# Softmax sums from ones beside the values, with head rows gathered by transfers, in a windowed attention and mixture-of-experts kernel

## The chip, the cores and the metric

The kernel runs on one core of a Trainium2 chip. TensorE multiplies matrices into PSUM, VectorE (DVE) and ScalarE (ACT) read PSUM and work on SBUF, GpSimd (POOL) works on SBUF and issues indirect transfers, SyncE (SP) issues the other transfers. The metric is the device time of one execution in microseconds, shown as the median of several runs.

## The reference

The input is 8 sequences of 1024 rows of 128 numbers. Cut to what matters:

```python
def attn(x, Wq, Wk, Wv, Wo):              # H = 16 heads of 8, window 64
    q, k, v = (split_heads(x @ w) for w in (Wq, Wk, Wv))
    scores = einsum('bhld,bhlwd->bhlw', q, k_win) * 8 ** -0.5   # row l sees rows l-63 .. l
    scores = where(invalid, -inf, scores)
    attn = softmax(scores, axis=-1)
    ctx = einsum('bhlw,bhlwd->bhld', attn, v_win)
    return ctx.reshape(Bx, Lx, 128) @ Wo

def ffn(x, w_router, w1, w2, bias):       # 8 experts, two of them for each row
    scores = softmax(xf @ w_router)
    expert_weights, top_experts = top_k(scores, 2)
    # rows go to their experts in order, up to a capacity of 2048 rows each
    h = gelu(einsum('ech,ehf->ecf', xb, w1))
    y = einsum('ecf,efh->ech', h, w2)
    return scatter_add(weight * y) + bias

x = x + attn(layernorm(x), Wq, Wk, Wv, Wo)
x = x + ffn(layernorm(x), w_router, w1, w2, bias)
```

What this change touches is the end of the attention: the product of the unnormalised probabilities P with the values (the numerators), the sums of P over the window (the denominators), and their quotient, ctx.

## The kernel before

A first phase computes attention and routing, a second one the experts; the second reads the rows that the first has scattered into the table xb, so it starts when the last of them has landed.

The first phase walks over 64 tiles of 128 rows: sequences b = 0 to 7, and in each tiles j = 0 to 7. Heads are held in four groups g of 32 partitions (a quad), four heads r to a quad. Iteration i of the loop at L1017 is one step; it does, in this order on each engine:

- scores of tile i+1 (L518 adds the mask, L534 the products), 128 rows x 96 columns for each head; then on DVE their maxima (L542) and two subtractions that split each maximum into BF16 pieces (L550);
- `attend` of tile i-1: 16 matmuls of P with the values (L620), 8 with a block of ones, obd, for the sums (L627). Both write one PSUM tile av. ScalarE copies it, keeping the even heads (L633), DVE adds the odd heads (L634), takes the reciprocal of the sums (L639) and multiplies (L640) into ctx;
- `probs` of tile i: masks (L579, L587), scores transposed (L596), then the turn of the maxima of tile i+1 (L559, copied by ScalarE at L561), then the subtraction of the maxima (L604) and the exponential on ScalarE (L610);
- the plan of this step: a list of calls written out by hand with `at(b, j, ...)` at L837 to L967. Among them are projections (`queries`, `keys`, `values`, `turn`) of the next sequence and the output projection, second normalisation and routing (`Piece`) of the sequence before. L904 `half` and L936 `piece` do the same for the two halves of the last two sequences.

The order on TensorE, DVE, ScalarE and POOL is the order in which the calls are written. SP's transfers are put into an order by the framework; a transfer that waits holds up those behind it on its queue. SP carries the loads of x, the spreading of queries and keys into their block layout (`spread`, L478 and L481), the copies of the values to the other half of the partitions (L467, L469) and the rows with bias (L704). POOL issues the indirect transfers to xb (`put`, L796), up to three in a step, each tied to a matmul of the step.

PSUM is tight: score tiles and probability tiles take turns in one pool of three buffers (ps_u, two tiles of each in a step); every other product (av, pm, projections) takes turns in a pool of two (ps_t).

After the loop the last tile is attended, the last two half sequences go through `piece`, the last rows are put, and 20 matmuls on the identity (L1049) stand before the expert phase.

## Time and profile before

| | |
|---|---|
| median of 15 runs | 767.72 us (765.59 to 769.61) |
| the profiled execution | 764.39 us |
| its span, first to last instruction | 762.5 us |
| mean granted TensorE clock | 0.962 |
| instructions | 23,372 |
| first expert products | 496 us |

Times inside the span are in microseconds from its start. Groups are listed by line, engine, operation and tiles (out<-in); after the count stand busy time, mean nanoseconds of one, and idle time of the engine just before them. In a timeline the columns are start, length, engine, line and operation, and in brackets the idle time before and what ended it; a merged row covers several instructions. FP32 matmuls are recorded as two instructions each, and matmuls of different quads run side by side, so the busy time of a group is less than its count by its mean.

### The profile page before, as it was taken

The numbers are of one execution on the slowest core, as the hardware profiler recorded it, in microseconds if no ns is written. First come the engines' busy times: TensorE is split into PE (matmuls) and PEld (weight loads), VectorE is DVE, ScalarE is ACT, GpSimd is POOL, SyncE is SP. The second block draws the span as 40 slices with busy tenths as digits, with TensorE's granted clock in tenths as the row PEclk, the third lists the DMA queues.
The fourth block names the chain that finished last, engine by engine and source line by source line (L and its number), as shares of the span: only waits on it lengthen the run. The fifth ranks groups of instructions, "written<-read, shape, count | busy, mean of one in ns | idle before, by whom it ended". The sixth has DMA issues, their size and how long they took to land.

```text
span 762.5 us, 23372 instructions
## 1 busy us (share of the span) xinstructions
PE 685.9 (90%) x9749; PEld 492.4 (65%) x9749; DVE 415.7 (55%) x1142; ACT 374.8 (49%) x665; POOL 394.8 (52%) x518
## 2 busy tenths in 40 slices
PE   8899999999999999999998872399999999999990
PEld 6455655655556546556555541389999999898990
DVE  6586778878888788888788777021111111111010
ACT  5465666675675666656655441023444444443430
POOL 7001030354543543444414556538778787787876
PEclk9999999999999999999999996689999999999995
DMA  2444445133123333232212111236455465463333
GB/s 79 128 143 144 148 141 187 36 98 98 48 88 98 92 94 93 88 90 66 83 58 56 47 45 60 81 92 107 50 113 106 46 123 94 52 119 34 37 32 30
DMA packets 66698, 65.25 MB, mean 86 GB/s; under 512 B 9043, under 2 KB 53944, under 8 KB 65696
## 3 DMA queue, kind: packets, MB, share of 16 engines
q1 hardware_dynamic: 39328, 38.08, 16.5%
q0 software_dynamic: 22528, 16.74, 15.5%
q10 hardware_dynamic: 4736, 8.93, 3.1%
q8 instruction: 77, 1.26, 0.7%
q14 instruction: 29, 0.24, 0.1%
HBM read 17.37 MB, written 29.88 MB: 62 GB/s over the span
## 4 chain that ended last, share of the span: by engine, by line
PE 65%; DVE 11%; POOL 8%; issue 7%; ACT 5%; DMA 3%; SPq 0%; POOLq 0%; ACTq 0%; DVEq 0%
PE yp L1118 11%; PE hp L1107 11%; PE av L620 7%; PE av L627 6%; PE t L596 6%; PE s L534 6%; POOL out_dram L1128 5%; ACT pr L610 3%; DVE mx L542 3%; PE pm L559 3%; PE s L518 2%; PE po L675 2%; PE pq L429 2%; PE t L604 2%; DMA out_dram<-ye,dest 2%
## 5 line engine op out<-in xcount | busy, mean ns | idle before, releaser
L1128 POOL DMA_INDIRECT out_dram<-ye,dest x128 | 198.6, 1552 | 68.4 <-issue 26.2
L796 POOL DMA_INDIRECT xb<-xn,si x128 | 126.4, 987 | 174.9 <-PE s L534 75.5
L542 DVE TENSOR_REDUCE mx<-s 128x8 f32<-128x768 f32 x128 | 116.5, 952 | 42.6 <-PE s L534 39.3
L1118 PEld LDWEIGHTS yp<-w,hT 128*128 128x128 f32 x1024 | 124.9, 193 | 9.1 <-ACT hT L1111 3.8
L1118 PE MATMUL yp<-w,hT 128*128 128x128 f32 x1024 | 126.2, 276 | 4.6 <-DVE ye L1123 3.9
L610 ACT ACTIVATE pr<-t 128x1024 f32<-128x1024 f32 x128 | 124.5, 1029 | 1.9 <-PE t L604 1.7
L1107 PE MATMUL hp<-xts,w 128*128 128x256 f32 (+1 forms) x528 | 123.3, 377 | 0.3 <-DVE xts L1098 0.3
L1123 DVE TENSOR_TENSOR ye<-yp,gt 128x256 f32<-128x256 f32 (+1 forms) x66 | 27.1, 415 | 162.7 <-PE yp L1118 122.7
L1111 ACT ACTIVATE hT<-hp 128x512 f32<-128x512 f32 x128 | 76.4, 597 | 71.8 <-PE hp L1107 66.9
L1107 PEld LDWEIGHTS hp<-xts,w 128*128 128x128 f32 x528 | 94.9, 194 | 10.1 <-DVE xts L1098 0.5
L620 PEld LDWEIGHTS av<-pr,vbd 128*32 128x32 f32 x2048 | 54.1, 110 | 47.1 <-issue 28.1
L620 PE MATMUL av<-pr,vbd 128*32 128x128 f32 x2048 | 73.4, 278 | 5.8 <-ACT pr L610 2.7
L633 ACT ACTIVATE own<-av,even 128x256 f32<-128x256 f32 x64 | 30.3, 474 | 94.1 <-PE av L627 94.1
L561 ACT COPY mxt<-pm 128x512 bf16<-128x512 bf16 x64 | 37.5, 586 | 78.4 <-PE pm L559 68.7
L596 PE MATMUL t<-qbd,kt 32*128 32x256 f32 x1024 | 69.6, 383 | 0.0
L627 PE MATMUL av<-pr,obd 128*32 128x256 f32 x1024 | 69.6, 383 | 0.0
L1098 ACT COPY xts<-xt 128x256 f32<-128x256 f32 (+1 forms) x57 | 21.0, 369 | 87.7 <-PE xt L1096 87.7
L639 DVE RECIPROCAL rd<-own 128x128 f32<-128x128 f32 x64 | 61.0, 953 | 2.2
L534 PE MATMUL s<-kbd,qt 32*32 32x384 f32 x2048 | 60.2, 493 | 1.4 <-issue 0.8
L596 PEld LDWEIGHTS t<-qbd,kt 32*128 32x128 f32 x1024 | 47.3, 187 | 3.3 <-issue 0.9
L518 PE MATMUL s<-ms,i 32*128 32x384 bf16 x256 | 34.2, 329 | 9.5 <-ACT pr L610 7.0
L627 PEld LDWEIGHTS av<-pr,obd 128*32 128x32 f32 x1024 | 35.7, 111 | 9.7 <-issue 0.7
(179 smaller groups left out, 782.1 us busy)
## 6 DMA issues: line engine op xcount, KB each, us to landing
xb<-zeros ACTq DMA_DIRECT2D x16, 528.0 KB
xe<-xb SPq DMA_DIRECT2D x7, 1056.0 KB
vbd<-vbd SPq DMA_DIRECT2D x32, 192.0 KB
kbd<-kt SPq DMA_DIRECT2D x62, 72.0 KB
qbd<-qt SPq DMA_DIRECT2D x64, 64.0 KB
out_dram<-x SPq DMA_DIRECT2D x32, 128.0 KB
w<-in_L_ffn_w_dram SPq DMA_DIRECT2D x16, 256.0 KB
x<-in_L_attn_x_dram SPq DMA_DIRECT2D x22, 128.0 KB
```

What stands on the lines that cost most here:

```text
L534: done = nc.tensor.matmul(place(g, slice(32 * blk, 32 * (blk + 1))), lhsT=qt[quad(g), q0 : q0 + 32], rhs=kbd[quad(g), :, c0 + 32 * blk : c ...
L542: nc.vector.tensor_reduce(out=part_of(mx, 0)[:, 2 * u : 2 * u + 2], in_=units[u][:, :, 0 : 4 * KB].rearrange("p g (r k) -> p g r k", r=4), ...
L596: nc.tensor.matmul(units[g // 2][:, g % 2, w], lhsT=kt[quad(g), q0 : q0 + P], rhs=qbd[quad(g), :, c0 : c0 + 64], start=False, stop=False, ...
L610: nc.scalar.activation(pr[:, 2 * u : 2 * u + 2], units[u], AF.Exp)
L620: begun = nc.tensor.matmul(av[quad(g), 0, w], lhsT=pair_values(2 * j + w, g, k), rhs=pr[:, g, w, 2 * k : 2 * k + 2, :], start=k == 0, stop ...
L627: last = nc.tensor.matmul(av[quad(g), 1], lhsT=obd[:, k, :], rhs=pr[:, g, :, 2 * k : 2 * k + 2, :], start=k == 0, stop=k == 1, skip_group_ ...
L639: nc.vector.reciprocal(rd, den)
L796: ins = nc.gpsimd.indirect_dma_start(out=xb[:, :], out_offset=bass.IndirectOffsetOnAxis(ap=slot, axis=0), in_=row, in_offset=None, bounds_ ...
L1107: nc.tensor.matmul(hp[:, c], lhsT=ws[e][0][:, (c0 + c) * P : (c0 + c + 1) * P], rhs=xt, start=True, stop=True,)
L1111: nc.scalar.activation(hT[:, c0 : c0 + per], hp, AF.Gelu_apprx_tanh)
L1118: nc.tensor.matmul(yp[:, k, :], lhsT=hT[:, c, k * P : (k + 1) * P], rhs=ws[e][1][:, c, :], start=c == 0, stop=c == NC - 1,)
L1128: add = nc.gpsimd.indirect_dma_start(out=acc, out_offset=bass.IndirectOffsetOnAxis(ap=dests[e][:, n : n + 1], axis=0), in_=ye[:, k, :], in ...
```

## The change

The values tile vbd gets, beside each pair of numerators, two columns of ones, so that one product of P with 32 columns yields the numerators of two heads and their sums; the eight matmuls with obd go away. The columns are laid out by head within a quad (value columns and rows of Wo are permuted to match: four transfers for Wo, a ScalarE copy for Wv). A pair's product writes, for both of its heads s, numerators and sums into its own place of av, of which each head needs only its own rows. ScalarE copies av whole into a tile `sums` for four tiles. A new class `Context` gathers the rows: four transfers bring the numerators of a group of tiles into ctx, and the sums go one of two ways. In groups of four tiles (`few`, the first half of sequences 0 to 5) they go to DRAM once per head, come back as 128 x 64, are inverted there, are written to DRAM and are read back with each row broadcast to the eight partitions of its head. In the other groups four transfers bring them already repeated into `den`, and the inversion is of the full width. `invert` and `scale` are called at the end of the step that issues the transfers, or one and three steps later for groups of four.

In `probs` the plan's calls up to its first product now stand ahead of the turn of the maxima. The mask matmul of the scores writes only the first and the last 32 of the 96 columns. Several calls of the plan move to other steps; the roots of the second normalisation go from POOL to DVE. The last tile keeps the old form (`attend_last`), with a values tile vend copied for it; after the loop the calls stand in another order, with 38 matmuls on the identity instead of 20.

```diff
-        ms = c1.tile([P, 4, KB], BF16, tag="ms", name="ms")
+        ms = c1.tile([P, 4, 2, 32], BF16, tag="ms", name="ms")
@@ scores
+                ends_of = place(g, slice(0, P))
+                ends_of = bass.AP(
+                    tensor=ends_of.tensor, offset=ends_of.offset,
+                    ap=[list(ends_of.ap[0]), [KB, 4], [64, 2], [1, 32]],
+                )
                 nc.tensor.matmul(
-                    place(g, slice(0, P)),
+                    ends_of,
...
@@ probs
+            for call, args in early:
+                call(*args)
             mxt_ahead = turn_max(*ahead) if ahead else None
...
@@ attend
             for w in range(2):
                 for k in range(2):
                     for g in range(NQ):
-                        begun = nc.tensor.matmul(
-                            av[quad(g), 0, w], lhsT=pair_values(2 * j + w, g, k),
+                        last = nc.tensor.matmul(
+                            av[quad(g), k, :, w], lhsT=pair_values(vbd, 2 * j + w, g, k),
+                            rhs=pr[:, g, w, 2 * k : 2 * k + 2, :], start=True, stop=True,
+                            skip_group_check=True, tile_position=(0, 32 * g),
+                        )
+                begun = last if w == 0 else begun
+            if j % 4 == 0:
+                sums[b, j // 4] = a2.tile([P, 4, 4, P], F32, tag="sums", name=f"sums_{b}_{j}")
+            nc.scalar.copy(
+                sums[b, j // 4][:, :, j % 4], av.rearrange("p k s w q -> p (k s) (w q)")
+            )
+            return begun, last
+
+        class Context:
+            def __init__(self, b, j0, n, few=False):
...
+                for r in range(4):
+                    nc.sync.dma_start(
+                        out=self.ctx[r::4], in_=av[r % 2 :: 4, r].rearrange("p t c -> p (t c)")
+                    )
+                if few:
+                    total = dram2.tile([4, NQ, 4 * P], F32, tag="total", name=f"total_{b}_{j0}")
+                    for r in range(4):
+                        nc.sync.dma_start(out=total[r], in_=av[4 * r + 2 + r % 2 :: 32, r])
+                    self.one = a2.tile([P, 64], F32, tag="one", name=f"one_{b}_{j0}")
+                    nc.sync.dma_start(
+                        out=self.one, in_=total.rearrange("r g (a c) -> (r g a) c", c=64)
+                    )
+                else:
+                    for r in range(4):
+                        nc.sync.dma_start(out=self.den[r::4], in_=av[2 + r % 2 :: 4, r])
+            def invert(self):
+                if not self.few:
+                    nc.vector.reciprocal(self.den, self.den)
+                    return
+                nc.vector.reciprocal(self.one, self.one)
...
+                for r in range(4):
+                    nc.sync.dma_start(
+                        out=self.den[r::4].rearrange("p t c -> p (t c)"),
+                        in_=inv[r].unsqueeze(1).to_broadcast([NQ, DH, 4 * P]),
+                    )
+            def scale(self):
+                nc.vector.tensor_tensor(
+                    self.ctx, self.ctx, self.den.rearrange("p t c -> p (t c)"), ALU.mult
+                )
@@ the plan, b from 1
-                at(b, 0, of, *f, "out", 3, 3)
-                at(b, 1, of, *f, "out", 6, 2)
+                at(b, 0, of, *f, "out", 3, 1)
...
-                at(b, 2, turn, b + 1, 0)
+                at(b, 1, turn, b + 1, 0)
                 at(b, 2, turn, b + 1, 1)
+            if b < 7:
+                at(b, 2, of, *f, "out", 4, 2)
+                at(b, 2, of, *f, "stats", range(2))
+                at(b, 3, of, *f, "out", 6, 2)
...
-                at(b, 3, keys, b + 1, 0)
+                at(b, 4, keys, b + 1, 0)
...
+        together = {}
+        for b in range(B):
+            for j0, n in ((0, 4), (4, 2), (6, 2)) if b < 6 else (
+                (0, 2), (2, 2), (4, 2), (6, 8 - b)
+            ):
+                together[b * NJ + j0 + n - 1] = (b, j0, n, n == 4)
@@ the loop
                 begun, _ = attend(*todo)
                 put(1 if b >= 5 else 0, begun)
-            pr, mxt, done = probs(b, j, mxt, ahead)
+                if i - 1 in together:
+                    context = Context(*together[i - 1])
+                    late[i + context.few].append(context.invert)
+                    late[i + 3 * context.few].append(context.scale)
+            n = next((n + 1 for n, step in enumerate(plan[i]) if is_product(*step)), 0)
+            pr, mxt, done = probs(b, j, mxt, ahead, plan[i][:n])
...
-            for call, args in plan[i]:
+            for call, args in plan[i][n:]:
                 call(*args)
-        go(ends[0], 3)
-        _, at_last = attend(*todo)
+            for call in late[i]:
+                call()
+        go(ends[0], 4)
+        at_last = attend_last(*todo)
...
-        after(stay_awake(20).ins, mark.ins)
+        after(stay_awake(38).ins, mark.ins)
```

## The prediction

> **What bounds the kernel now.** I read the slices first, then the groups of instructions, then the timeline of a few tiles, and last the transfer queue and the clock windows. In the slices and the totals:
>
> ```profile
> PE 685.9 (90%) x9749; PEld 492.4 (65%) x9749; DVE 415.7 (55%) x1142; ACT 374.8 (49%) x665; POOL 394.8 (52%) x518
> PE   8899999999999999999998872399999999999990
> DVE  6586778878888788888788777021111111111010
> ```
>
> A slice is 19 us. Attention is the first 24 slices (to about 458 us), TensorE full in all of them; then comes a gap in which the last rows are routed and scattered, then the expert stage, which the change leaves alone. What the change takes away is in the groups:
>
> ```profile
> L627 PE MATMUL av<-pr,obd 128*32 128x256 f32 x1024 | 69.6, 383 | 0.0
> L639 DVE RECIPROCAL rd<-own 128x128 f32<-128x128 f32 x64 | 61.0, 953 | 2.2
> L634 DVE SCALAR_TENSOR_TENSOR own<-av,odd,own 128x256 f32<-128x256 f32 x64 | 30.8, 482 | 13.3 <-ACT own L633 5.6 <-issue 5.5
> ```
>
> A busy TensorE need not be the limit, so the timeline decides. Tile 5 to 6 of the second sequence:
>
> ```profile
> 108.19 0.40 PE L559 MATMUL pm<-ident_b,mx 128*128 128x128 bf16 x4
> 108.68 0.59 ACT L561 COPY mxt<-pm 128x512 bf16<-128x512 bf16 x1 [1.09 <-PE pm L559]
> 109.16 1.95 ACT L610 ACTIVATE pr<-t 128x1024 f32<-128x1024 f32 x2
> 110.24 0.34 PE L518 MATMUL s<-ms,i 32*128 32x384 bf16 x2 [0.17 <-ACT pr L610]
> 110.51 0.93 PE L534 MATMUL s<-kbd,qt 32*32 32x384 f32 x32
> 111.37 1.10 PE L620 MATMUL av<-pr,vbd 128*32 128x128 f32 x32
> 112.27 1.06 PE L627 MATMUL av<-pr,obd 128*32 128x256 f32 x16
> 113.26 0.40 PE L579 MATMUL t<-i,mt 32*128 32x256 bf16 x8
> 113.49 1.03 PE L596 MATMUL t<-qbd,kt 32*128 32x256 f32 x16
> 114.46 0.40 PE L559 MATMUL pm<-ident_b,mx 128*128 128x128 bf16 x4
> ```
>
> The reader is to see a loop. The score tile and the probability tile share three PSUM buffers, so the second half of the next scores (L518 at 110.24) waits for the first exponential, which stands on ScalarE behind the copy of the turned maxima, which waits for pm. From pm (108.19) to the next L534 (110.51) it is 2.32 us, whatever TensorE has to do. From L534 to pm TensorE needs 0.86 + 0.90 + 0.99 + 0.23 + 0.97 = 3.95 us. The loop is 6.27 us, and steps with one projection take 6.27 (116.17 to 122.44). Two projections after pm make a step TensorE's own: 7.38. The eight steps j = 0 to 7 of sequence 3 (starts of L518, from 181.60) are 6.85, 6.01, 6.19, 7.38, 5.77, 6.80, 6.27 and 7.48, in sum 52.75 us.
>
> **What the change removes from a step.** L627 costs 0.99 us of TensorE; the mask matmul falls from 384 to 256 columns, by a third of 0.27 = 0.09. DVE loses 0.48 + 0.95 + 0.30. The copy of av on ScalarE goes from 474 ns to 512 columns, 605 ns by the L443 row; it follows the exponential with room. Without L627 pm comes earlier, but two things now stop it. T's second half reuses the buffer of the first score unit, so it waits for the first maximum: L534 + 1.08 + 0.95 + 0.07 = 2.1 instead of 1.76, which puts pm at 3.2. And the subtractions must be done: 1.08 + 1.82 + 0.42 + 0.1 = 3.4.
>
> **What it moves.** The first product of each plan step now stands ahead of pm, in the loop, instead of behind it, where the 2.32 us hid it. So pm = 3.2 + E, and the step is 3.2 + E + 2.32; where E's result is copied by ScalarE ahead of the maxima (queries, keys, turns), 0.3 more. E from the rows: an output projection or value tile 0.265 each, a turn of four 0.53, keys or queries 0.96, count 0.54. Steps 0 to 7: E = 0.80 (6.3), 0.53 (6.1), 0.53 (6.8: its buffer and the sums copy stand behind four normalisations of 0.50 and the earlier turn on ScalarE), 0.53 (6.05), 0.96 (6.8), 0.96 (6.9, also behind four normalisations), 0.96 (6.8), 0.54 plus the padding mask (6.2). Sum 51.95 against 52.75. The microsecond taken from each tile is given back, because it was taken from a loop into which the products were put. What remains are the steps of 7.38 and, in the last two sequences, crowded ones of 8 to 10 us. Read off in the same way, sequence 0 takes 54.7 before, 1 to 5 together 264.0, 6 takes 55.7 and seven steps of 7 take 49.0; against them stand 52.7 (its own plan), 5 x 51.9, 51.9 and 7 x 6.0 (few products there), in sum **-17**.
>
> **What it adds.** For each group of tiles four transfers bring the numerators, four the sums, then DVE inverts and scales. In the groups of two (the second half of sequences 0 to 5, all of 6 and 7: 20 groups with the last of one tile) `invert` is called at the end of the very step that issues the transfers, and DVE works in order: behind it stand the maxima of the next tile. The transfers' price is in the queue's timeline:
>
> ```profile
> 178.62 2.43 SPq L481 DMA_DIRECT2D kbd<-kt  x4
> 181.15 2.45 SPq L478 DMA_DIRECT2D qbd<-qt  x4
> ```
>
> These are the nearest kin, 32 strided partitions to 32: eight issues from 178.62 to 183.60, 0.56 to 0.64 us apart; the semaphore records put a landing 1.75 to 1.9 us after its issue. In the new step, av ends at 1.9, the copy at 2.6, the first issue is at 2.7, the eighth at 2.7 + 7 x 0.6 = 6.9, landed at 8.7. A reciprocal of 256 columns isn't in the trace; 128 columns take 0.95 and 4 columns 0.18, so 1.75 by the line through both (bounds 0.95 and 1.9). With the scaling (0.42 by the 256-column L680) DVE is free at 11.1. The next maxima could have begun at 6.3 + 1.08 = 7.4: they are 3.7 late (3.3 with the fastest issues). T and pm wait for them, so TensorE stands, and nothing behind makes up for it, since every step is already at its loop. Fourteen groups: 14 x 3.7 = 52.
>
> In sequences 0 to 5 the group of tiles 4 and 5 is worse. The compact path of tiles 0 to 3 has left on the same queue a write of the inverted sums that waits for DVE's reciprocal (about 6.6 us into step 5), then broadcasts that wait for that write (1.8 us) and take 0.6 each: the queue is free 4.7 to 5.1 us into step 6 instead of at 2.7. That is 2 more: 6 x 5.7 = 34, **+86** in all. In up to three sequences the queue also holds result rows that wait for POOL's bias additions ahead of this group (0 to 4 us each; I take 0, as the additions usually end first).
>
> The compact path itself delays no engine: its reciprocal stands one step later and its scaling three. The transfers of keys, queries and values share the queue but have a step or more to spare (60 issues of 0.6 us, 36 us of a sequence's 60).
>
> **The end.** The last group (tile 6) is inverted before choose and count of the first half, and count now stands on TensorE ahead of the last attention product: 8.7 + 1 + 2 against 5.5 before, **+5** (0 to 10); the scatter that follows is paced by POOL at 1.28 us a row and is as long as before. The longer wake-up matmuls lie in the wait for the first expert rows.
>
> **The clock.** Two windows of the trace:
>
> ```profile
> 425.20:428.60 3.40, 1.89 (x40) 0.84 (x40) 2.89 (x15) 2.43 (x3) 0.97 (x1) 1.00 0.12 40
> 428.60:432.00 3.40, 3.40 (x64) 2.34 (x48) 2.27 (x5) 1.77 (x5) 1.94 (x2) 0.50 0.08 25
> ```
>
> TensorE was busy 1.89 of 3.40 us, and for the next 3.4 us the granted clock was 0.50; L620 and L627 took 1.95 and 1.87 instead of 1.10 and 1.06. A stall of 3.7 to 5.7 us does the same. The half-rate stretch costs 0 (it lies in the wait) to 1.7 us (all of it on the path): 0 to 34 us for 20 stalls. I take 1.7 for the six long ones, which hold a whole idle window, and 0 for the rest: **+10**.
>
> The Trainium skill, "TensorE: Matmul & The Clock Gate" (section "Why this matters for your kernels"), allows gaps up to about 3 us before the clock falls. The rows are stricter: two windows of attention that were 0.51 (from 22.4) and 0.56 busy lowered it, with no gap over 1.9 us. By the rule all 20 stalls count, +34 instead of +10. The page "DMA: Bandwidth & Descriptors" (section "Rules for kernel authors") says to issue a transfer early and wait for it late; the new groups of two wait at once, which speaks against them.
>
> **Sum.** 764.4 (the profiled execution: span 762.5 and 1.9 around it) - 17 + 86 + 5 + 10 = 848; the median of the runs lies 3.3 above that execution, so 851. The slope of the reciprocal and the issue spacing both lean down (3.3 for 3.7: -8), so I say **843**.
>
> **Rivals.** *Faster.* The transfers land before DVE would need them, or the stalls are hidden by slack I don't see: then -17 remains, 750, and if the loop also gave way to TensorE's own work all of 64 x 1.08 = 69 us, 699. It needs a group to cost under 17/20 = 0.85 us, so sums usable 5 us after their copy instead of 8.5. For it: the issue slots of plain loads are 0.37 us. Against: eight slots and one landing are 4.4 us even then, before any reciprocal. Chance 0.13. *Half the stall.* Issues at 0.37 and the short reciprocal: 1.2 to 2 us a group, 24 to 40 us, no clock loss: about 785. Chance 0.12. *The clock decides.* Steps with E = 0.96 and nothing after pm leave TensorE 1.7 us idle in one stretch, a window half busy; if two steps of each sequence and all stalls fall to half rate, 851 + 24 + 16 x 1.7 = 900. Chance 0.13. *The new ones-beside-values product does not replace L627 at equal cost*: 16 matmuls stay 16, same columns, so nothing speaks for it; under 0.02. My forecast has 0.6.
>
> **Range.** 785 to 900 leaves the faster case and the far end of the clock case outside. 0.2% (1.5 us) is what a measurement of this kernel can tell from no change. Faster 0.14, same 0.01, slower 0.85.
>
> **What would show it.** DVE waits of 3 to 6 us whose releaser is a transfer into den, twice in each of sequences 0 to 5 and four times later; TensorE waiting at T (now L596) for the maxima right after; gaps of 4 to 6 us there with clock 0.5 behind them; steps without a stall at 6.0 to 6.9; L627's 69.6 us gone. I am wrong if den's waits are under 1 us, or if the steps fall to 5.5 us.

## The result and the profile after

The changed kernel takes **923.68 us** (median of 12 runs, 919.71 to 928.4), the kernel before 767.16 us (62 runs): a ratio of **1.204**, 95% interval 1.2027 to 1.2061. It is slower by 157 us. The forecast was 843 us, in a range of 785 to 900: the direction was right, the size was half of what came, and the time lies outside the range. The profiled execution after has a span of 922.9 us and a mean granted clock of 0.869 (before: 762.5 and 0.962).

The kernel before took 765 to 768 us in three sets of runs (that of the result among them) and 752 to 753 us in four others, at the same granted clock of 0.96 and on one and the same chip in both ways, for a reason that is not known, so each kernel is given with its ratio to the kernel before in its own set, and differences between times of different sets carry that 2%.

The page of the changed kernel, its totals and three rows of its 40 slices (here 23 us each):

```profile
PE 704.8 (76%) x8777; PEld 507.6 (55%) x8777; DVE 361.7 (39%) x1088; ACT 382.9 (41%) x670; POOL 374.1 (41%) x430
...
PE   7895694795796796786677777620899999999992
...
DVE  6442463564554555453635565561111111110110
...
PEclk9897797799799799799878787765899999999997
```

TensorE issues 972 instructions fewer, yet is busy 19 us longer, and its row, mostly nines in attention before, is full of sixes and sevens; the clock row dips in the same slices. DVE has lost 54 us of work and is no faster for it. What TensorE waits for stands in the groups (instruction, count, busy us and mean ns, then idle time ahead of it and what ended it) and in the waits (engine and line, what it waited for, us in total, times, longest):

```profile
L596 PE MATMUL t<-i,mt 32*128 32x256 bf16 x448 | 39.6, 309 | 97.7 <-DVE mx L559 96.8
...
L613 PE MATMUL t<-qbd,kt 32*128 32x256 f32 x1024 | 99.3, 462 | 1.0 <-issue 0.6
...
L644 PE MATMUL av<-pr,vbd 128*32 128x128 f32 x2016 | 77.6, 292 | 3.3 <-ACT pr L629 1.8
...
L685 DVE RECIPROCAL den<-den 128x256 f32<-128x256 f32 (+1 forms) x20 | 34.2, 1712 | 103.3 <-DMA den<-sums 99.0
```

```profile
DVE den L685 <- DMA den<-sums: 99.0, 18, 12.8
PE t L596 <- DVE mx L559: 96.8, 21, 7.2
```

This is the chain that was forecast, link by link: DVE waits 99 us for sums to land, and TensorE waits 97 us at the probability tile (t) for maxima that stand behind that wait. L644, the product with the ones beside the values, is busy 77.6 us, where L620 was 73.4 and L627, which is gone, 69.6. One stall in sequence 4, from the timeline of the changed kernel (start, busy us, engine, instruction; in brackets the idle time before and its releaser):

```profile
307.04 1.58 PE L551 MATMUL s<-kbd,qt 32*32 32x384 f32 x32
...
310.53 0.59 ACT L652 COPY sums<-av 128x512 f32<-128x512 f32 x1 [2.97 <-PE av L644]
...
311.14 2.42 SPq L668 DMA_DIRECT2D ctx<-sums  x4
...
313.66 2.45 SPq L681 DMA_DIRECT2D den<-sums  x4
...
314.55 0.93 PE L551 MATMUL s<-kbd,qt 32*32 32x384 f32 x32
...
317.43 1.75 DVE L685 RECIPROCAL den<-den 128x256 f32<-128x256 f32 x1 [3.27 <-DMA den<-sums]
...
319.21 0.42 DVE L699 TENSOR_TENSOR ctx<-ctx,den 128x256 f32<-128x256 f32 x1
319.55 1.82 DVE L559 TENSOR_REDUCE mx<-s 128x8 f32<-128x768 f32 x2
320.56 0.61 PE L596 MATMUL t<-i,mt 32*128 32x256 bf16 x6 [3.84 <-DVE mx L559]
320.76 2.12 PE L613 MATMUL t<-qbd,kt 32*128 32x256 f32 x16
```

The scores at 314.55 are done by 315.5 and their maxima could start at 315.6; they start at 319.55, because DVE, in order, first waits for eight transfers issued between 311.1 and 316.1. Then L613 takes 2.12 us, where at full clock this kernel's L613 takes 1.13 (at 68.53). The clock windows of the same stretch (window, its length, busy us and instructions of TensorE, its weight loads, DVE, ScalarE, POOL, then the granted clock, the share of DMA and GB/s):

```profile
313.50:316.90 3.40, 2.85 (x72) 1.40 (x72) 0.36 (x2) 3.21 (x6) 1.77 (x2) 1.00 0.24 76
316.90:320.30 3.40, 0.00 (x0) 0.00 (x0) 2.84 (x3) 0.59 (x1) 0.00 (x0) 0.84 0.07 21
320.30:323.70 3.40, 3.14 (x26) 2.49 (x26) 1.45 (x4) 0.00 (x0) 0.00 (x0) 0.50 0.02 5
323.70:327.10 3.40, 3.40 (x50) 1.71 (x49) 1.51 (x5) 2.77 (x5) 0.97 (x1) 0.66 0.28 70
```

TensorE idles for most of a window, and from the end of that window on the clocks add up to 6.8 us at half rate (1.1, 3.4 and 2.3), with TensorE busy in all but the first 1.4 of them. From 40 us to the last attention product the half rate holds for 184 us, before for 3.4.

By stage, in us from the span's start (before, after): last attention product 459.1, 613.3; last scattered row 490.2, 648.1; first expert product 496.5, 660.6; span 762.5, 922.9. Attention is 154.2 longer, what lies between it and the experts 9.9, the expert stage 3.7 shorter.

### The profile page after: what moved, and what is told of

It is laid out like the page before. It is cut to its first block, busy times and chain, and to the rows that moved or that the text cites. A ratio compares the mean times of both kernels' runs of the same rounds, so it can differ in the third digit from the quotient of the medians.

```text
span 922.9 us, 21704 instructions
## 1 busy us (share of the span) xinstructions
PE 704.8 (76%) x8777; PEld 507.6 (55%) x8777; DVE 361.7 (39%) x1088; ACT 382.9 (41%) x670; POOL 374.1 (41%) x430
## 3 DMA queue, kind: packets, MB, share of 16 engines
q8 instruction: 69, 1.13, 0.5%
## 4 chain that ended last, share of the span: by engine, by line
PE 40%; issue 18%; POOL 11%; SPq 8%; DMA 8%; DVE 7%; ACT 6%; POOLq 1%; another core or an unknown queue 0%; ACTq 0%; DVEq 0%
POOL out_dram L1256 7%; PE t L613 6%; PE yp L1246 6%; PE hp L1235 6%; PE av L644 4%; PE s L551 3%; ACT pr L629 3%; POOL xb L888 3%; SPq L681 3%; PE t L596 3%; DMA den<-sums 2%; SPq L668 2%; DVE mx L559 2%; DVE den L685 2%; PE pv L463 2%
## 5 line engine op out<-in xcount | busy, mean ns | idle before, releaser
L596 PE MATMUL t<-i,mt 32*128 32x256 bf16 x448 | 39.6, 309 | 97.7 <-DVE mx L559 96.8
L613 PE MATMUL t<-qbd,kt 32*128 32x256 f32 x1024 | 99.3, 462 | 1.0 <-issue 0.6
L644 PEld LDWEIGHTS av<-pr,vbd 128*32 128x32 f32 x2016 | 57.6, 116 | 49.7 <-issue 42.0
L652 ACT COPY sums<-av 128x512 f32<-128x512 f32 x63 | 36.9, 586 | 113.4 <-PE av L644 68.0
L644 PE MATMUL av<-pr,vbd 128*32 128x128 f32 x2016 | 77.6, 292 | 3.3 <-ACT pr L629 1.8
L596 PEld LDWEIGHTS <-mt 32*128 32x128 bf16 x448 | 11.6, 94 | 117.2 <-issue 113.8
L685 DVE RECIPROCAL den<-den 128x256 f32<-128x256 f32 (+1 forms) x20 | 34.2, 1712 | 103.3 <-DMA den<-sums 99.0
L613 PEld LDWEIGHTS t<-qbd,kt 32*128 32x128 f32 x1024 | 70.3, 230 | 6.2 <-issue 5.3
L551 PE MATMUL s<-kbd,qt 32*32 32x384 f32 x2048 | 65.2, 539 | 5.6 <-DMA kbd<-kt 5.6
L535 PE MATMUL s<-ms,i 32*128 32x256 bf16 x256 | 33.6, 290 | 30.3 <-ACT pr L629 23.1
```

The source lines that it names most:

```text
L551: done = nc.tensor.matmul(place(g, slice(32 * blk, 32 * (blk + 1))), lhsT=qt[quad(g), q0 : q0 + 32], rhs=kbd[quad(g), :, c0 + 32 * blk : c ...
L596: nc.tensor.matmul(to, lhsT=mt[quad(g), 0, hq, :], rhs=i32[quad(g)].rearrange("p (w r) q -> p w r q", w=2), start=hq == 0, stop=False, ski ...
L613: nc.tensor.matmul(units[g // 2][:, g % 2, w], lhsT=kt[quad(g), q0 : q0 + P], rhs=qbd[quad(g), :, c0 : c0 + 64], start=False, stop=False, ...
L644: last = nc.tensor.matmul(av[quad(g), k, :, w], lhsT=pair_values(vbd, 2 * j + w, g, k), rhs=pr[:, g, w, 2 * k : 2 * k + 2, :], start=True, ...
L685: nc.vector.reciprocal(self.den, self.den)
```

## The experiments

The eight steps from j = 0 of sequence 4, in us between the starts of the score masks; in sequence 4 the changed kernel stalls in the second and the eighth. The forecast was made for sequence 3.

```
                 j=0    1     2     3     4     5     6     7    sum
before           6.91  6.01  6.19  7.38  5.77  7.50  6.27  7.48  53.5
forecast         6.3   6.1   6.8   6.05  6.8   6.9   6.8   6.2   52.0 (no stalls)
after            6.98 12.35  5.79  6.70  7.87  5.86  6.82 15.31  67.7
e3_early_only    7.82  6.64  6.32  7.91  5.90  7.68  7.43  8.83  58.5
e1_later         7.56  6.15  7.86  6.70  6.85  5.61  6.71  7.73  55.2
e5_later_plain   8.24  5.65 12.95  6.29  7.49  5.76  6.00  6.34  58.7
e6_all           9.08  5.83  7.94  6.19  7.54  5.45  6.10  6.54  54.7
e8_two_later     5.51  5.98  5.72 11.65  7.65  5.34  5.68  6.15  53.7
e9_..._early     5.97  6.15  6.32  6.70  6.85  5.53  6.71  7.76  52.0
e12_third_apart  5.54  5.99  7.12  7.16  7.54  5.34  5.68  6.16  50.5
```

**e1_later: take the wait out of the step that issues it.** The changed kernel, sequences 0 to 6:

```diff
-                    late[i + context.few].append(context.invert)
-                    late[i + 3 * context.few].append(context.scale)
+                    wait = 1 if context.few or together[i - 1][0] < 7 else 0
+                    late[i + wait].append(context.invert)
+                    late[i + (3 if context.few else wait)].append(context.scale)
```

> The changed kernel, with invert and scale of the groups of two called one step later in sequences 0 to 6 (16 of the 20 groups); the transfers stay where they are, the last sequence keeps its four stalls. Theory (DVE waits in order for the transfers, the next maxima stand behind it, TensorE stalls and falls to half clock): a stalled step of the changed kernel lasts 13.6 us on average against 6.2 without a stall, so 16 x 7.4 = 118 us go: about 806 us, the DVE wait for den falls from 99 us to under 30, half-rate windows all but vanish before the last sequence. Rival (the added transfers and the fuller queue slow the steps themselves, or the products ahead of the maxima do): the stalls only move, and the time stays above 880.

Measured: 819.56 us, ratio 1.0911 (1.087 to 1.0952); the last attention product at 500.1 instead of 613.3; half rate 51 instead of 184 us. The waits of this run:

```profile
PE t L596 <- DVE mx L559: 19.1, 14, 5.0
...
DVE den L685 <- DMA den<-sums: 9.6, 7, 2.4
```

More than half of the loss hangs on where two calls stand: 0.113 of 0.204 by the ratios, 113 of 154 us of attention in the profiled execution (811.79 us, 8 below the median). The table shows it: 12.35 and 15.31 become 6.15 and 7.73, and of the others only the third grows by more than a microsecond (7.86, where the moved reciprocal now stands).

**e2_warm: keep the clock up in the stalls.** Identity products that the masks behind them overwrite:

```diff
+            for _ in range(fill):
+                nc.tensor.matmul(
+                    units[0][:, 0].rearrange("p w r q -> p (w r q)")[:, 0:P],
+                    lhsT=ident, rhs=ident, start=True, stop=True, skip_group_check=True,
+                )
...
+            held = i - 2 in together and not together[i - 2][3]
+            pr, mxt, done = probs(b, j, mxt, ahead, plan[i][:n], 18 if held else 0)
```

> The changed kernel, with 18 matmuls on the identity (about 4 us at full clock) put into each stalled step ahead of the masks of the transposed scores, where TensorE would stand still; their output is overwritten. The stalls stay, the clock should not fall. Theory (a stall costs its own 5.5 us and then about 2 to 2.6 us more through the half-rate windows behind it): 19 x 2 to 2.6 = 38 to 50 us less, about 880. Rival (the clock does not matter since TensorE is not the limit of a step): within 8 us of the changed kernel's 924, or slower by what the fillers overrun.

Measured: 890.33 us, ratio 1.183 (1.1799 to 1.1861); the span is 34 us shorter than after's, by the ratio it would be 16 us. The second step of sequence 4 takes 10.18 instead of 12.35 us. The kernel before took 753.04 us in this set, 2% less than in the set of the result, so this bounds the clock's part but doesn't settle it (see e13_warm_more).

**e3_early_only: the product ahead of the turn, alone.** The kernel before, with the change's order of products and nothing else of it:

```diff
-            pr, mxt, done = probs(b, j, mxt, ahead)
+            n = next((n + 1 for n, step in enumerate(plan[i]) if is_product(*step)), 0)
+            pr, mxt, done = probs(b, j, mxt, ahead, plan[i][:n])
...
-            for call, args in plan[i]:
+            for call, args in plan[i][n:]:
```

> The kernel before, with one part of the change alone: the calls of the plan up to the first product stand ahead of the turn of the maxima. Theory (the product then lies inside the loop from the scores through the maxima and the exponential to the next scores, where 2.32 us of cover are lost): a step is 3.95 + E + 2.32, 0.3 more where ScalarE copies the product first; eight steps sum to about 57 against 52.75, so 30 us more, about 797. Rival (the product fills a wait for DVE's maxima, so it is free or gains): 755 to 768.

Measured: 812.95 us, ratio 1.0785 (1.0737 to 1.0832): 60 us, twice what was expected. The sequence is 58.5 us. The step j=6 of the table, from 305.73 to 313.16 (6.27 us before, 7.43 here), in this run's timeline:

```profile
305.38 0.60 ACT L435 ACTIVATE qt<-pq 128x512 f32<-128x512 f32 x1 [1.76 <-PE pq L429]
...
305.88 0.58 ACT L561 COPY mxt<-pm 128x512 bf16<-128x512 bf16 x1
...
306.34 1.96 ACT L612 ACTIVATE pr<-t 128x1024 f32<-128x1024 f32 x2
...
307.44 0.34 PE L518 MATMUL s<-ms,i 32*128 32x384 bf16 x2 [1.38 <-ACT pr L612]
307.70 0.93 PE L534 MATMUL s<-kbd,qt 32*32 32x384 f32 x32
...
311.65 1.13 PE L442 MATMUL pk<-xnt,wk_sb 128*128 128x512 f32 x2
312.61 0.39 PE L559 MATMUL pm<-ident_b,mx 128*128 128x128 bf16 x4
```

On ScalarE the copy of the queries' result (305.38) stands ahead of that of the maxima (305.88), so the scores wait 1.38 us for the exponential, where 0.17 was usual before; and the keys (0.96 us, 311.65) stand ahead of pm on TensorE. With L627 still in the loop there is nothing that pays for either.

**e4_den_first: sums before numerators.** The changed kernel with the four transfers of the sums issued ahead of the four of the numerators.

> The changed kernel, with the four transfers of the sums issued ahead of the four of the numerators in the groups of two. Theory (DVE's wait is the issue time of eight transfers and one landing, then reciprocal, then scaling): den lands 4 x 0.62 = 2.5 us earlier, the reciprocal of 1.75 us then runs while the numerators land, and the scaling comes 1.75 us earlier: 20 x 1.75 = 35 us less, about 889, a little less still if half-rate windows go. Rival (the wait is set by something ahead of these transfers on the queue, or by landing alone): within 10 us of 924.

Measured: 873.02 us, ratio 1.16 (1.157 to 1.163); by ratios 34 us less than after, by the last attention product (560.8 for 613.3) 52. The waits of this run:

```profile
DVE den L690 <- DMA den<-sums: 44.0, 12, 8.9
...
DVE ctx L704 <- DMA ctx<-sums: 21.6, 16, 2.4
```

DVE's waits for sums and numerators fall from 99.0 to 65.6 us, 33 less, and that agrees with the ratios and with the 35 expected: the reciprocal now runs while the numerators land, and the scaling waits for these. The order of the issues is part of the lateness; the 52 us carry the 2% between sets and a shorter half rate (135 us for 184).

**c_after, e5_later_plain, e6_all, e7_awake20, in one set.**

> The changed kernel unaltered, on the same chip as the three kernels beside it. If chips differ only by a common factor, the ratio to the kernel before is again 1.20 to 1.21. If it is off by more than 0.01, comparisons made by ratios across chips carry that much error.

Measured: 925.87 us, ratio 1.2048 (1.1983 to 1.2113).

e5_later_plain is e1_later with no product ahead of the turn:

```diff
-            n = next((n + 1 for n, step in enumerate(plan[i]) if is_product(*step)), 0)
+            n = 0
```

> The changed kernel with the groups of two inverted one step later (as e1_later), and with the first product of each step back behind the turn of the maxima. Theory (the early product lies in the loop of scores, maxima, turn, exponential, and is paid in full): the step falls from 3.2 + E + 2.32 to the larger of 5.8 us and TensorE's own sum; a sequence falls from the 55.2 us of e1_later to 47 to 50, and the kernel from a ratio of 1.091 to 1.02 to 1.04, 35 to 50 us below e1_later. Rival A (TensorE would only stand waiting for DVE's maxima ahead of the turn, so that the early product is free): a sequence stays at 54 to 56 us and the ratio at 1.08 to 1.10. Rival B (with no early product TensorE idles before pm for over 1.5 us in each step and the clock falls): half-rate stretches in attention over 100 us and a ratio above 1.10.

Measured: 824.07 us, ratio 1.0745 (1.0689 to 1.0801). The theory's number fell, and the ratio came close to Rival A's, but not for Rival A's reason. Five of the eight steps stand at 5.65 to 6.34 us (in e1 at 5.61 to 7.73); the three others rose to 7.5 to 13. The worst, from this run's timeline:

```profile
264.03 2.46 SPq L681 DMA_DIRECT2D den<-sums  x4
...
267.94 1.75 DVE L685 RECIPROCAL den<-den 128x256 f32<-128x256 f32 x1 [3.34 <-DMA den<-sums]
269.73 0.43 DVE L699 TENSOR_TENSOR ctx<-ctx,den 128x256 f32<-128x256 f32 x1
270.07 1.82 DVE L559 TENSOR_REDUCE mx<-s 128x8 f32<-128x768 f32 x2
271.07 0.61 PE L596 MATMUL t<-i,mt 32*128 32x256 bf16 x6 [4.85 <-DVE mx L559]
```

One step of delay is not enough when steps get shorter: the same stall is back. Early product and stall had been mixed.

e6_all is e5_later_plain with the sums first, the last two groups late as well (the very last one inverted behind the loop), the last attention product ahead of the last count, and 20 wake-up products:

```diff
+                    late[i + 1].append(context.invert)
+                    late[i + (3 if context.few else 1)].append(context.scale)
...
-        go(ends[0], 4)
+        go(ends[0], 1)
+        for call in late[len(tiles)]:
+            call()
         at_last = attend_last(*todo)
+        go(ends[0], 3)
...
-        after(stay_awake(38).ins, mark.ins)
+        after(stay_awake(20).ins, mark.ins)
```

> As e5_later_plain, and besides: sums gathered ahead of numerators, the last two groups of sequence 7 also inverted one step later (the last of them after the loop), the last attention product ahead of the last count, 20 instead of 38 wake-up matmuls before the experts. Theory (what is left are the stalls of the two groups at the end and the half-rate wake-up): 12 to 20 us below e5_later_plain, a ratio of 0.99 to 1.02. Rival (the steps, not the stalls, hold what remains): within 6 us of e5_later_plain.

Measured: 794.37 us, ratio 1.0333 (1.028 to 1.0386), 30 us below e5_later_plain: more than either side expected, and still above the theory's ratio, since the stalls inside the sequences had been counted as gone and were not (9.08 and 7.94 in the table).

e7_awake20 is the changed kernel with only the wake-up products cut.

> The changed kernel with 20 instead of 38 wake-up matmuls between the last scatter and the first expert. Theory (38 at half clock run 6 us past the arrival of the first expert rows): last put to first expert product falls from 12.5 to about 6.5 us, the time by 6 us, a ratio 0.008 lower than the control's. Rival (the rows arrive late anyway; or the 18 more matmuls earn their time back by a faster clock in the expert stage): within 2 us of the control, or the expert stage longer by as much as the tail is shorter.

Measured: 923.18 us, ratio 1.2025 (1.195 to 1.2099), which tells nothing apart by itself; the trace does. The wake-up and the first expert product, of the changed kernel:

```profile
649.21 10.88 PE L169 MATMUL awake<-ident 128*128 128x128 f32 x76 [23.73 <-issue]
...
660.63 1.16 PE L1235 MATMUL hp<-xts,w 128*128 128x128 f32 x8 [0.33 <-DVE xts L1226]
```

and of e7_awake20:

```profile
652.41 6.86 PE L169 MATMUL awake<-ident 128*128 128x128 f32 x40 [23.69 <-issue]
...
659.81 1.16 PE L1235 MATMUL hp<-xts,w 128*128 128x128 f32 x8 [0.33 <-DVE xts L1226]
```

Last scattered row to first expert product: 12.5 us after (11.9 in c_after), 8.5 here, 6.3 before. So 3.4 of the expected 6. The rest is where the wake-up starts: 1.1 us behind the last scattered row, in both; in the kernel before it started 5.3 us ahead of it (484.97 and 490.23), since there five rows were scattered behind the mark that it waits for. In the changed order of the ends no row is left behind the mark.

**e8_two_later and e9_two_later_early, in one set.** e6_all with the groups of two inverted two steps after their transfers, and ahead of that step's other calls:

```diff
+                    wait = 2 if i < 59 and not context.few else 1
+                    late[i + wait].append(context.invert)
+                    late[i + (3 if context.few else wait)].append(context.scale)
...
-            for call, args in plan[i][n:]:
-                call(*args)
             for call in late[i]:
                 call()
+            for call, args in plan[i][n:]:
+                call(*args)
```

> As e6_all, and the groups of two are inverted two steps after the one that issues their transfers instead of one, ahead of that step's other DVE work instead of behind it. Theory (what e6_all still loses are the same stalls, moved into the steps after: T waits there for maxima that stand behind a reciprocal of 1.75 us and its transfers; the loop without them is 5.5 to 6.3 us): the wait of DVE for den falls below 3 us, a sequence falls from 53 to 63 us to 47 to 52, the last attention product from 486 to 445 to 465 us, the kernel to a ratio of 0.97 to 1.00. Rival (the steps are long because DVE, ScalarE and the transfer queue are crowded in them, whatever the sums wait for): within 10 us of e6_all, a ratio of 1.02 to 1.04.

Measured: 757.42 us, ratio 1.0056 (1.0026 to 1.0087); the last attention product at 452.3, den's waits 6.3 us in all, sequences (divided as in the table) of 48.0 to 54.0 us but for sequence 0 (56.8). 0.199 of the ratio's 0.204 are gone, with the transfers, the compact inversion and the ones beside the values in place; the first product of a step is back behind the turn here, and e9 tells its part from that of the stalls. What is left in sequences 3 to 5 is one step of 9.5 to 11.9 us each (in 5 a second one of 9.2); that of sequence 4:

```profile
246.93 2.45 SPq L677 DMA_DIRECT2D den<-sums  x4
249.43 2.50 SPq L679 DMA_DIRECT2D ctx<-sums  x4
...
252.03 0.64 SPq L479 DMA_DIRECT2D vbd<-vbd  x1
...
252.71 1.42 SPq L481 DMA_DIRECT2D vbd<-vbd  x1
...
255.91 1.51 PEld L644 LDWEIGHTS av<-pr,vbd 128*32 128x32 f32 x32 [4.28 <-issue]
```

The attention product stands 4.28 us until shifted values have come that were issued behind eight gathers. The profile calls its releaser "issue"; the order of the queue, and e10_values_apart below, name the transfer.

> As e8_two_later, but with the first product of each step ahead of the turn of the maxima again, as in the change. Theory (that product is paid in the loop, and in the runs so far the price was mixed with the stalls): 0.5 to 1.0 us more in each of some 55 steps, a ratio 0.035 to 0.07 above e8_two_later. Rival (it only fills a wait of TensorE for DVE): within 0.01 of e8_two_later.

Measured: 769.19 us, ratio 1.0216 (1.0183 to 1.0249), 11.8 us above e8_two_later: between the two. It has the change's order of products too, so 0.183 of the 0.204 go with the place of the waits and the edits of e6_all, of which the sums first is the largest (e4_den_first). In sequences 2 and 6, where e8_two_later has no long step, the early product costs 4.4 and 2.6 us (52.4 and 52.0 for 48.0 and 49.4); in 3 to 5 it delays the attention product until the values are there, and so hides a wait of nearly its own size.

**e10_values_apart and e12_third_apart: the shifted values on another queue.** In e10 all shift transfers of the values are issued by ScalarE (`nc.sync.dma_start` becomes `nc.scalar.dma_start` at both), in e12 only those of the third value tile, behind the copy of the turned rows.

> As e8_two_later, and the two shift transfers of each value tile are issued on ScalarE's queue instead of SP's (six a sequence, ScalarE pays each issue, 0.58 us by the two it issues in the kernel before); the compact sums of sequence 0 are inverted one step later. Theory (the steps of 9 to 13 us that e8_two_later has left, one each in sequences 1, 3, 4 and 5, are waits of the attention product or the scores for shifted values and spread keys that stand in SP's queue behind the eight transfers of a group): no step above 8.5 us in sequences 1 to 5, a sequence at 48 to 50 us, 15 to 25 us less than e8_two_later, a ratio of 0.97 to 0.99. Rival (the six issues of 0.58 us on ScalarE stand in the loop ahead of the turned maxima's copy): the steps with values grow by 0.5 to 1.2 us, 12 to 20 us in all, and the ratio stays at 1.00 to 1.02.

Measured: 767.37 us, ratio 1.0182 (1.016 to 1.0204). Both sides were half right. The three long steps are gone (11.88, 11.65 and 9.46 become 6.18 or 6.19), and the others grew, as the rival said; one, in sequence 1:

```profile
95.87 0.63 ACTq L479 DMA_DIRECT2D vbd<-vbd  x1
...
96.54 1.02 ACTq L481 DMA_DIRECT2D vbd<-vbd  x1
...
99.17 0.56 ACT L431 COPY xnt<-tp_x 128x512 f32<-128x512 f32 x1
...
99.78 0.38 PE L576 MATMUL pm<-ident_b,mx 128*128 128x128 bf16 x4 [1.54 <-ACT xnt L431]
```

> As e8_two_later, but only the two shift transfers of the third value tile of sequences 1 to 7 are issued on ScalarE's queue, behind the copy of the turned rows. Theory (e10_values_apart showed that the steps of 9 to 12 us in sequences 3 to 5 are the attention product's wait for these shifted values; its loss came from the issues of the other two value tiles and from standing ahead of that copy): those three steps fall from 11.9, 11.7 and 9.5 to about 6.2 us, no other step grows by over 0.3 us, 10 to 15 us below e8_two_later, a ratio of 0.985 to 0.995. Rival (1.2 us of issues on ScalarE delay the sums copy and through it the next product in every sequence): 5 us or more come back in the steps with tiles 2 to 4, a ratio of 0.995 to 1.01.

Measured: 752.89 us, ratio 1.0003 (0.9986 to 1.0021), the fastest here and the same as the kernel before. The three steps fall to 7.2 to 7.5, not 6.2, and the step ahead of each grows by 1.4 to 1.9.

**c2_after and e13_warm_more, in one set:** what of a stall is lateness, and what is the clock. e13 is e2_warm with 26 or 20 identity products in place of 18. Other than its expectation says, nothing of the computation is changed: the masks behind the identity products overwrite what they write.

> The changed kernel unaltered, once more, as the partner of e13_warm_more on one chip, and because the kernel before took 767 to 768 us on some of the chips and 752 to 754 us on others. If that 2% belongs to the chip, the changed kernel shows it too and the ratio stays at 1.20; if it belongs to the kernel before alone, the changed kernel stays near 924 us whatever the chip, and on a chip where the kernel before takes 753 the ratio is 1.22 to 1.23.

Measured: 923.95 us, ratio 1.2074 (1.2039 to 1.2109), with the kernel before at 764.91. This is the chip on which the kernel before took 752.49 us in the set of e8_two_later, so the 2% doesn't belong to the chip. What the changed kernel takes where the kernel before takes 753 stays open.

> As e2_warm, with 26 identity matmuls in the steps stalled by the group of tiles 4 and 5 of sequences 0 to 5 and 20 in the other stalled steps (they write into score buffers, so the output isn't the reference's). Theory (each stall costs the lateness of the maxima, some 5.5 us, and 2 to 2.5 us of half rate behind it): half-rate stretches in attention fall from 184 to under 50 us, attention gets 35 to 50 us shorter than the partner's, the rest of the stalls' price, over 100 us, stays. Rival (the half rate is most of the price): attention over 70 us shorter. Other rival (the clock costs little, its stretches lie in waits): under 20 us shorter.

Measured: 901.0 us, ratio 1.1774 (1.1614 to 1.1935), the two executions 906.13 and 895.87. Attention in windows from 75 to 560 us, first c2_after, then e13_warm_more:

```profile
75.00:560.00 485.00, 355.67 (x5690) 209.99 (x5691) 247.37 (x690) 223.15 (x380) 118.59 (x179) 0.85 0.27 84
```

```profile
75.00:560.00 485.00, 425.60 (x6703) 282.98 (x6707) 260.91 (x731) 230.54 (x398) 124.48 (x185) 0.97 0.28 86
```

The clock goes from 0.85 to 0.97, the half rate from 181 to 53 us, and attention is 19.5 us shorter in the profiled execution; the other execution is 10 us shorter still. So the gain is 20 to 30 us: below the theory's 35 to 50, with the profiled execution just inside the rival that the clock costs little (under 20), and far from the rival that the half rate is most of the price (over 70). Scaled from the 127 us taken away to all 181, an estimate of 28 to 42 us for the clock: a fifth to under a third of what the stalls cost. The filling products take TensorE's time too, so the clock's part may be somewhat larger.

## Why the forecast had the mechanism right and the size half

**Right: the mechanism and its places.** Four signs came: den's waits behind a transfer (though 1.2 to 12.8 us long instead of 3 to 6), TensorE at T (L596) behind the maxima, half clock behind that, L627 gone. The stalls stand in the steps that were named: two in each of sequences 0 to 5, more in 6 and 7. The fifth, steps without a stall at 6.0 to 6.9 us, came in part: in sequence 4 they take 5.8 to 7.9. e1, which moves nothing but the place where DVE waits, takes back more than half of the loss; e9, which also gathers the sums first and changes the order at the end, takes back 0.183 of the ratio's 0.204. The Trainium skill, "DMA: Bandwidth & Descriptors" ("Rules for kernel authors"), says to issue early and wait late; these runs price the opposite at about 7 us for each wait (the 18 stalled steps of attention take 264 us in after and 134 in e9).

The forecast's sum against what was measured, in us:

| term | forecast | measured | from |
|---|---|---|---|
| steps without stalls | -17 | +4 | 63 steps of attention, e9 427.0, before 423.0 |
| stalls, lateness and clock | 86 + 10 | 143 | the same 63 steps (18 of the 20 stalls), after 570.2, less e9 427.0 |
| the end | 5 | 7 + 9.9 | attention's 154.2 less 147.2 in the steps (the other two stalls); from there to the experts |
| expert stage | 0 | -3.7 | its length before and after |
| sum | 84 | 160 | span 922.9 less 762.5 |

**The step that failed most is the +86 and the +10, "14 x 3.7 + 6 x 5.7" and "1.7 for the six long ones": 143 instead of 96.** *Lateness.* I put the maxima 4.8 us behind the start of their scores, 6.8 for tiles 4 and 5. In the first 18 stalls of the changed kernel they start 5.0 to 8.4 us behind it: 7.5 in the mean after tiles 4 and 5 of sequences 0 to 5, 6.4 in the others. Less the 1.08 us that they need anyway, 12 x 5.3 + 6 x 6.4 = 102, where the forecast for these 18 was 12 x 3.7 + 6 x 5.7 = 79. The reciprocal was as estimated (1.75 by the line, 1.75 measured). What was short is what stands ahead of it: landing came 1.9 to 3.6 us after the last issue (1.8 taken), and the copy of the sums later than 2.6 us, 4.1 in the stall shown above, where the half rate left by the stall before still stretched the scores. The trace before already had the long landings: by its semaphore records 49 of 121 transfers of keys and queries landed 2.2 to 4.4 us after their issue, and of the eight that the prediction reads the last took 3.9 (183.00 to 186.93); a wait for several transfers ends with the slowest of them. Taking 8 us off for leaning down was wrong too.

*The clock.* Of the 143, 130 lie in the 18 stalled steps and 13 in the others, into which the half rate runs on. That leaves 28 in the stalled steps and 41 in all for the clock and smaller things, which agrees with the 28 to 42 estimated from e13. I had let only six long stalls pay. In the runs every one does: DVE's order makes each stall of these steps a gap of 3.6 us or more on TensorE, and each has a stretch of 6.8 us or more at half rate around or behind it. The Trainium skill, "TensorE: Matmul & The Clock Gate" ("Why this matters for your kernels"), draws its line at gaps of about 3 us; by it all 20 stalls counted and the term was +34. That rule was nearer than my reading of two windows.

**The -17 failed as well, by 21 us.** Its core held: I had said that the microsecond taken from each tile is given back by the product put into the loop. Sequences 3 and 4 of e9, with that product and without stalls, take 51.98 us each, and 51.95 was forecast; that this is so close is partly luck, as single steps are up to 1.6 us off. Without the early product sequence 2 of e8 takes 48.0: the move costs 3 to 4 us a sequence here, and 60 us in all where nothing pays for it (e3). What I had wrong was the edges, sequences 0, 1 and 7. The last step of sequence 0, in which the scores of sequence 1 begin, takes 14.2 us in e9 and 20.2 in after (7.7 before). The timeline of the changed kernel there:

```profile
67.85 2.06 SPq L693 DMA_DIRECT2D den<-one_873i  x3
...
73.25 1.81 SPq L493 DMA_DIRECT2D kbd<-kt  x3
...
77.72 1.59 PE L551 MATMUL s<-kbd,qt 32*32 32x384 f32 x32 [4.47 <-DMA kbd<-kt]
```

The compact path's broadcasts stand in SP's queue ahead of the spread of the next sequence's keys, and the scores wait 4.47 us for these. I had written that this path "delays no engine". In sequence 1 it holds up ScalarE too, by the profile's releaser:

```profile
ACT sums L652 <- DMA den<-one_1732i: 7.2, 1, 7.2
```

ScalarE stands until 150.23 us, and the seventh step of sequence 1 takes 12.9 us (8.7 in e9, 6.3 before); no run takes this wait out alone. And sequence 7 takes 49.4 instead of 42, probably as its products and not the loop set its steps; that isn't tested.

**The end was forecast at 5 and took 17.** The 7 us lie where the last group and the count were named (0 to 10): behind the last step attention takes 18.4 us before, 25.6 after and 16.0 in e9, where the last inversions stand later and the last product stands ahead of the count. That "the longer wake-up matmuls lie in the wait for the first expert rows" is refuted by e7: they start behind the last row, 18 of them cost 3.4 us, and their late start most of the other 2.8 of the 6.2. Three more rows are left to scatter (28 for 25), 3.8 us at POOL's 1.28.

**The rivals.** *Faster* needed sums usable 5 us after their copy; even in the stall shown above, the mildest of the 18, they took 6.3 (311.1 to 317.4). *Half the stall* needed issues of 0.37 and a reciprocal of 0.95; they are 0.59 and 1.75. *The clock decides* gave a nearer time (900) with the clock as its cause; the clock is 28 to 42 of 160, lateness 102, so it is no better as an explanation. That the ones beside the values cost more than L627 is refuted by the groups: L644 is busy 77.6 us, for 73.4 and 69.6 of L620 and L627 before, and steps without waits go down to 5.3 us (e8).

Three readings of the prediction were loose without moving its sum: the 24 slices of attention before are 7 to 9 tenths busy, not full in all; 851 + 24 + 16 x 1.7 is 902, not 900; and a sequence takes some 52 us, not 60.

What stays open: why the kernel before differs by 2% between sets, and with it the exact share of the steps (e9 and the profile of before are of different sets); the split of the last 7 us of attention between the last group and the count.

## What to carry to other kernels

A wait on an engine that works in order costs whatever stands behind it, not what stands ahead of it: put the instruction that needs a transfer behind the work that others wait for, and count the steps from the issue to the landing in the new, shorter steps, since one step was enough in e1 and not in the shorter ones of e5. Work moved within a loop must be priced against the loop, not against the engine's total: here a product moved by three lines cost 60 us alone. And a transfer added to a queue delays those behind it on that queue, so look for who waits for them; moving them to a compute engine's queue only helps where that engine has nothing urgent behind.

## What the hardware showed that was not expected

- Filling a stalled TensorE with idle products brought the granted clock from 0.85 to 0.97 and took 23 us of 924 (2.5%) off the time, though 127 us less were spent at half rate, which would be 64 us if all of it had set the end.
- In e10 an issue on ScalarE's queue is mostly 0.6 us of ScalarE's own order, and at times 0.8 to 1.9 (1.02 at 96.54), with the copy that TensorE needs behind it; on SP the same issues cost 0.6 us of the queue, and 4.3 us of TensorE when eight gathers stood ahead.
- A wait of the weight load for a transfer can appear as "issue" in the profile (4.28 us at 255.91): only the queue's timeline names it.
